# A seventh split step, denominators by square transposes and an earlier range check in the last image's second layer

## The chip, the cores and the metric

The kernel runs on one core of one Trainium2 chip. The metric is the device time of one execution in microseconds. The kernel before takes 3158.69 us, the median of three runs (3158.46 to 3160.62). One execution under the profiler took 3155.92 us, and its span in the trace, from the first to the last instruction, is 3154.1 us.

## The reference

Two attention layers, each with a residual, on four images of 4096 tokens and 256 channels, all in float32:

```python
# layer 0: q, k have 32 columns, v has 256
q, k, v = x @ Wq + bq, x @ Wk + bk, x @ Wv + bv
x = gamma * (softmax(q @ k.T) @ v) + x
# layer 1: f, g have 32 columns, v has 128; Wo brings 128 back to 256
f, g, v = x @ Wf + bf, x @ Wg + bg, x @ Wh + bh
out = x + (softmax(g @ f.T) @ v) @ Wo + bo
```

The softmax runs over the 4096 keys of the image. The kernel doesn't subtract a maximum: it takes exp of the scores, sums products and exponentials, and divides at the end. A range check at the end of the program counts denominators, values and gamma that are out of range; only if there are any does a general path run, and with these inputs it doesn't.

## The kernel before, in words

**Layers, blocks, steps.** For each image `b` and each layer `l` the queries are taken in blocks, and for each block the kernel goes through the keys in steps. In layer 0 a block has 256 queries and 8 steps of 512 keys (16 blocks). In layer 1, the one that is changed, a block has 512 queries and 16 steps of 256 keys (8 blocks, numbered 0 to 7 here). A class `Step` holds one step.

**One step of layer 1.** TensorE makes the scores `st` (L532): two products of 128 keys by 512 queries in the fast fp32r form. ScalarE takes the exponential from them, `p` (L544). TensorE then multiplies `p` with the values of these keys (L600), and the result adds up in PSUM over the steps of the block. This product comes in two forms.

- A *whole* step multiplies `p` by `v` in full float32, in two matmuls which stand as four in the trace.
- A *split* step, those in `SPLIT1`, does it in three products in fp32r, six matmuls in all. ScalarE also makes `high`, a slightly smaller exponential (L542); VectorE makes `low` from `p` and `high` (L555) and `d` from `low` and `high` (L560). The values have parts `h`, `l`, `d` of their own, made when the values are projected (L472 to L483). The products of `high` and `low` go to the accumulator acc0, those of `d` and of the whole steps to acc1.

**The denominators.** They are the sums of `p` over the keys. VectorE adds the `p` of eleven of the sixteen steps into `p_sum` (L571 the first two, L573 the others). The five steps of `MOVED_SUMS` are summed by accumulating transfers on GpSimd's queue (L548, L550) into a tile of tag "e".

**The end of a block.** ScalarE takes acc0 out into `o` (L651). `end_second` adds acc1 (L657), adds the moved sums to `p_sum` (L659) and halves it to `sums`, 128 partitions by 512 queries (L660): what is left is a sum over partitions. Then come four output units, one for each 128 queries, which run in the next block's steps 1 to 4: TensorE multiplies `o` by `Wo` (L667) and `sums` by a column of ones (L668), VectorE takes the reciprocal (L670), ScalarE scales (L673), and GpSimd's queue adds the result to the output in memory (L675).

**Buffers.** Tag "t" has two buffers, for `high` and `p` of split steps; tag "l" two, for `low` and `d`; tag "p" three, for `p` of whole steps; "d" and "e" one each, for the two sums; "small" four, among them those of `y`. In PSUM the scores of even and odd steps have one buffer each.

**What sets the order.** `plan` (L702 to L732) says at which step which units of the block before, and projections of the next image, are put. The loop over the steps (L735 to L802) writes a step as: `d` of this step, `low` of the next, the addition to `p_sum`, the scores of the step after the next (L775), the units of this step (L776), and the products of this step; the `d` product of a split step comes behind the product of the step after it (L778 to L783). The last step of a block takes acc0 out first (L774). The framework's scheduler then arranges the instructions of each engine from the dependencies and places in this order, so the built program's order is near to the written one and not the same.

**The end of the program.** After the last block's units the range check runs on VectorE: two comparisons and a product over all 256 columns of reciprocals, `inverse` (L808 to L810, in a "small" buffer), the check of values and gamma (L811 to L814), two reductions (L817), and then a count on TensorE (L821) which becomes the flag `off` (L822). The flag is read by the engines and a branch follows.

Of the kernel before, what the change touches and what calls it, by code (L numbers as in the profile page):

```python
# [57 lines left out]
P = 128  # L58
# [8 lines left out]

SPLIT1 = (0, 3, 5, 8, 11, 13)
MOVED_SUMS = (0, 4, 7, 9, 12)

# [168 lines left out]
def fast_path(ctx: ExitStack, tc: tile.TileContext, x, w0, w1, wo, bo, gamma, out, off):  # L239
# [11 lines left out]
    NI = (N // (G[0] * P), N // (G[1] * P))  # L251
    NS = QB0 // P
    NH = N // QB0
    split = [[l == 0 or i in SPLIT1 for i in range(NI[l])] for l in range(2)]
    V1 = NI[1] - sum(split[1])

    const = ctx.enter_context(tc.tile_pool(name="const", bufs=1))
    data = ctx.enter_context(tc.tile_pool(name="data", bufs=1))
# [30 lines left out]


    x_nat = {}
    LEAD_BUFS = sum(split[1])
    LEAD = V1 // NS

    def load_first(h):
# [11 lines left out]
    make_identity(nc, ident)  # L307
    ones = const.tile([P, 1], F32, name="ones")
    nc.vector.memset(ones, 1.0)

    inverse = const.tile([P, 2, B * N // P], F32, name="inverse")
    seen_v = const.tile([P, 2, B * NH], F32, name="seen_v")
# [99 lines left out]
    def project_units(b, l, h):  # L412

        key = (b, l, h)
        j, part = divmod(h, 2)
        cols = slice(part * QB0, (part + 1) * QB0)

        def qk_unit():
            ps = side_psum(f"psqk_{b}_{l}_{h}")[:, :QB0]
            for c in range(NCC):  # L420
                for n in range(2):
                    nc.tensor.matmul(  # L422
                        ps,
                        wqk[l][:, c, :],
                        x_parts[key][n][:, c, :],
                        start=(c == n == 0),
                        stop=(c == NCC - 1 and n == 1),
                    )
# [12 lines left out]
            nc.scalar.copy(parts[top, :], whole)  # L441
            nc.vector.tensor_sub(parts[bottom, :], whole, parts[top, :].bitcast(F32))

            if part == 0:
                qk_dram[b, l, j] = dram.tile([2, 2, D, QB], F32, name=f"qk_dram_{b}_{l}_{j}")
            nc.sync.dma_start(qk_dram[b, l, j].rearrange("h w d n -> (h w d) n")[:, cols], parts.bitcast(F32))
            halves[b, l, j] = part + 1
            if l == 0 and b > 0:
                load_half(b, h + 1)
            elif l == 1 and h == NH - 1:  # L450
                load_half(b + 1, 0)
            elif l == 1:
                load_squares((b, 1, h + 1), waiting.pop((b, h + 1)))
            if b == l == 0:
                near = parts.rearrange("(h w d) n -> h w d n", h=2, w=2)
                load_k(b, l, j, cols, near)
                if h == 0:
                    load_q(b, l, j, cols, near)

        def v_unit():  # L460
            ps = side_psum(f"psv_{b}_{l}_{h}")[:, : NS * CV[l]].rearrange("p (t c) -> p t c", c=CV[l])
            for t in range(NS):
                for c in range(NCC):
                    nc.tensor.matmul(  # L464
                        ps[:, t, :],
                        xT[key][:, c, t * P : (t + 1) * P],
                        wv[l][:, c, :],
                        start=(c == 0),
                        stop=(c == NCC - 1),
                    )  # L470
            seen = seen_v[:, l, b * NH + h : b * NH + h + 1]
            if split[l][h if l == 1 else 0]:  # L472
                if l == 0:
                    tiles = slice(part * NS, (part + 1) * NS)
                    high, low, d = (v0[j][what][:, tiles, :C] for what in ("h", "l", "d"))
                else:
                    t = data.tile([P, 3 * NS, P], F32R, tag="v1_parts", bufs=sum(split[1]), name=f"v_{b}_{h}")
                    high, low, d = (t[:, n * NS : (n + 1) * NS, :] for n in range(3))
                    v_t[b, h] = {"h": high, "l": low, "d": d}
                nc.scalar.activation(high, ps, AF.Copy, scale=1.0 - DOWN)  # L480
                nc.scalar.activation(low, ps, AF.Abs, accum_out=seen)
                nc.vector.scalar_tensor_tensor(d, high.bitcast(F32), -1.0 - EPS, ps, ALU.mult, ALU.add)
                nc.vector.scalar_tensor_tensor(low, d.bitcast(F32), UP, high.bitcast(F32), ALU.mult, ALU.add)  # L483
            else:
# [29 lines left out]
    class Step:  # L514


        def __init__(self, b, l, j, i):
            self.b, self.l, self.j, self.i = b, l, j, i
            self.first, self.last = i == 0, i == NI[l] - 1
            self.split = split[l][i]  # L520
            self.key = f"{b}_{l}_{j}_{i}"

        def scores(self):
# [18 lines left out]
                nc.scalar.activation(self.high, s_flat, AF.Exp, bias=down)  # L542
            self.p = wide("t" if self.split and l == 1 else "p", f"p_{self.key}")
            nc.scalar.activation(self.p, s_flat, AF.Exp)  # L544
            if l == 1 and i in MOVED_SUMS:
                if i == MOVED_SUMS[0]:
                    moved_sums[b, j] = wide("e", f"p_sum_moved_{b}_{j}")
                    nc.gpsimd.dma_start(moved_sums[b, j], self.p)  # L548
                else:
                    nc.gpsimd.dma_start(moved_sums[b, j], self.p, accum_op=ALU.add)  # L550
# [11 lines left out]
                )  # L562

        def add_up(self, p_sum):
            if self.l == 0 or self.i in MOVED_SUMS:
                return
            kept = [i for i in range(NI[1]) if i not in MOVED_SUMS]
            if self.i == kept[0]:
                first_p.append(self.p)
            elif self.i == kept[1]:  # L570
                nc.vector.tensor_add(p_sum, first_p.pop(0), self.p)  # L571
            else:
                nc.vector.tensor_add(p_sum, p_sum, self.p)  # L573
# [16 lines left out]
        def products_second(self, acc, parts):  # L590
            v = v_t[self.b, self.i]
            for part in parts:
                p, v_part, which, first, last = {
                    "h": lambda: (self.high, v["h"], 0, self.i == SPLIT1[0], False),
                    "l": lambda: (self.low, v["l"], 0, False, self.i == SPLIT1[-1]),
                    "d": lambda: (self.d, v["d"], 1, False, False),
                    "whole": lambda: (self.p, v, 1, self.i == 1, self.last),
                }[part]()
# [55 lines left out]
    def end_second(b, j, acc, p_sum, o):  # L654
# [3 lines left out]
        sums = work.tile([P, QB], F32, tag="sums", bufs=1, name=f"sums_{key}")  # L658
        nc.vector.tensor_add(p_sum, p_sum, moved_sums[b, j])  # L659
        nc.vector.tensor_add(sums, p_sum[:, :QB], p_sum[:, QB:])  # L660

        def output(t):
            def issue():
# [4 lines left out]
                nc.tensor.matmul(ps[:, C : C + 1], sums[:, tok], ones[:, :1], start=True, stop=True)  # L668
                n = (b * N + j * QB) // P + t
                nc.vector.reciprocal(inverse[:, 1, n : n + 1], ps[:, C : C + 1])  # L670
# [5 lines left out]

            return issue

        return [output(t) for t in range(NT)]

    def run(units):
        for u in units:
            u()


    x_res = {}
# [15 lines left out]
    def plan(b, l, j, ends):  # L702
# [3 lines left out]
        def put(i, *some):  # L706
            units.setdefault(i, []).extend(some)
# [15 lines left out]
        else:  # L723
            for n, u in enumerate(ends):
                put(1 + n, u)
        if b + 1 < B:
            for h in range(NH):
                i = 12 + 7 * h - j * NI[1]
# [72 lines left out]
        if s.last:  # L801
            ends = end_first(b, j, acc) if l == 0 else end_second(b, j, acc, p_sum, o)  # L802
    run(ends)

    good = small("good").rearrange("p (l n) -> p l n", l=2)
    nc.vector.tensor_scalar(good, inverse, 1.0 / SUM_MAX, None, ALU.is_ge)  # L808
    nc.vector.tensor_scalar(inverse, inverse, 1.0 / SUM_MIN, None, ALU.is_le)
    nc.vector.tensor_mul(good, good, inverse)  # L810
    nc.vector.tensor_scalar(seen_v, seen_v, VALUE_MAX, None, ALU.is_le)  # L811
    size = const.tile([P, 1], F32, name="size")
    nc.vector.tensor_mul(size, gamma_sb, gamma_sb)
    nc.vector.tensor_scalar(size, size, GAMMA_MAX**2, None, ALU.is_le)  # L814
    low = const.tile([P, 1], F32, name="low")
    for seen, axes in ((good, AX.XY), (seen_v, AX.XY)):
        nc.vector.tensor_reduce(low, seen, axes, ALU.min)  # L817
        nc.vector.tensor_mul(size, size, low)
    nc.vector.tensor_scalar(low, size, 1.0, None, ALU.is_lt)
    count = ps_side.tile([1, 1], F32, tag="side", name="count")  # L820
    nc.tensor.matmul(count, ones, low, start=True, stop=True)  # L821
# [51 lines left out]
```

## Time and profile before

| what | us |
|---|---|
| median of three runs | 3158.69 |
| the profiled execution | 3155.92 |
| its span in the trace | 3154.1 |
| TensorE busy | 3116.3 |
| VectorE busy | 2689.1 |
| ScalarE busy | 2140.1 |
| GpSimd busy | 900.7 |
| a block of the last image's second layer (`d` of step 0 at 3030.17, 3065.68, 3101.20) | 35.5 |
| from the flag (L822, starts at 3143.53) to the end of the span | 10.6 |

In the lines of the profile, PE is TensorE, PEld its loads of weights, which overlap its products, DVE VectorE, ACT ScalarE, POOL GpSimd and SP SyncE. A line of the timeline has a start and a duration in us, the engine, the line of the kernel, the operation, the tiles it writes and reads, their shapes, and how many instructions it stands for; square brackets give the idle time of the engine just before it and who ended it. A line of the groups has the busy time and the mean of one in ns, then the idle time before the group by who ended it. The rows of stretches have the busy time of each engine in that stretch, with its number of instructions.

The recorded duration of an instruction is a little longer than the distance from it to the next, since neighbours overlap; where costs are added up, it is done with these distances from start to start. The ends of matmuls are modelled.

### The profile page before, as it was taken

What the parts mean: (1) busy time and instruction counts of PE and PEld (TensorE: products, weight loads), DVE (VectorE), ACT (ScalarE), POOL (GpSimd) and SP (SyncE); (2) the same over time, 40 slices, a digit from 0 to 9 for tenths busy, and PEclk for the clock granted to TensorE, in tenths of its full rate; (3) what the DMA queues carried; (4) which work ended last, traced back from release to release, by engine and by line L of the source; (5) the groups of instructions that cost most, each with busy time, mean ns of one, the idle gap of its engine ahead of it and who ended that gap; (6) DMA issues with size and microseconds to landing.
All of it is one profiled execution on the core that took longest, in us unless ns stands there. A gap on an engine that the chain in (4) does not pass through costs nothing.

```text
span 3154.1 us, 54090 instructions
## 1 busy us (share of the span) xinstructions
PE 3116.3 (99%) x19908; PEld 2672.0 (85%) x19908; DVE 2689.1 (85%) x3237; ACT 2140.1 (68%) x2835; POOL 900.7 (29%) x1108
## 2 busy tenths in 40 slices
PE   8999999999999999999999999999999999999997
PEld 7999998666799999866679999976668999996664
DVE  7888888888888888888888888898888888888876
ACT  7666666777666666777766666677776666666674
POOL 5232224222422222422242222232223222233221
PEclk9999999999999999999999999999999999999999
DMA  4121114555512121555541112255554111125454
GB/s 119 43 53 47 48 48 104 107 108 105 104 44 51 41 53 47 113 101 112 107 93 47 49 45 51 51 116 107 105 113 81 48 46 47 49 65 105 97 95 73
DMA packets 391392, 239.49 MB, mean 76 GB/s; under 512 B 266672, under 2 KB 355248, under 8 KB 391120
## 3 DMA queue, kind: packets, MB, share of 16 engines
q0 software_dynamic: 68160, 134.86, 22.0%
q1 hardware_dynamic: 322048, 100.76, 13.4%
q8 instruction: 161, 2.64, 0.4%
q14 instruction: 111, 0.91, 0.1%
q10 hardware_dynamic: 912, 0.33, 0.1%
HBM read 82.58 MB, written 67.11 MB: 47 GB/s over the span
## 4 chain that ended last, share of the span: by engine, by line
PE 91%; DVE 3%; DMA 2%; issue 2%; ACT 1%; POOL 0%; SPq 0%; DVEq 0%; ACTq 0%; POOLq 0%
PE acc L600 24%; PE acc L582 23%; PE acc_pair L582 23%; PE st L532 14%; PE psv L464 4%; PE psqk L422 2%; PE pso L667 2%; DVE d L560 1%; DVE low L555 1%; ACT p L544 1%; DVE p_sum L573 1%; DMA p_sum_moved<-p 0%; DMA squares<-in_x 0%; PE pso L668 0%; DMA squares<-x_dram 0%
## 5 line engine op out<-in xcount | busy, mean ns | idle before, releaser
L542 ACT ACTIVATE high<-st,down 128x1024 fp32r<-128x1024 f32 x704 | 786.5, 1117 | 703.2 <-PE st L532 362.8
L544 ACT ACTIVATE p<-st 128x1024 f32<-128x1024 f32 x1024 | 1042.5, 1021 | 166.3 <-PE st L532 143.8
L560 DVE SCALAR_TENSOR_TENSOR d<-low,high 128x1024 fp32r<-128x1024 f32 x704 | 871.0, 1237 | 227.0 <-PE acc_pair L582 223.7
L555 DVE TENSOR_TENSOR low<-p,high 128x1024 fp32r<-128x1024 f32 x704 | 936.6, 1330 | 142.6 <-ACT p L544 141.6
L532 PE MATMUL st<-q,k 128*128 128x256 f32 (+1 forms) x3072 | 706.3, 338 | 2.5 <-DMA k<-qk_parts 1.4
L600 PE MATMUL acc<-p,v 128*128 128x512 f32 x1280 | 611.0, 597 | 0.0
L532 PEld LDWEIGHTS st<-q,k 128*128 128x128 f32 x3072 | 470.0, 189 | 103.3 <-issue 40.6
L639 POOL TENSOR_TENSOR x_res<-x,bo 128x256 f32<-128x256 f32 x128 | 212.5, 1660 | 879.3 <-DVE x L628 879.2
L600 PEld LDWEIGHTS acc<-p,v 128*128 128x128 f32 x1280 | 233.1, 189 | 161.8 <-issue 143.4
L573 DVE TENSOR_TENSOR p_sum<-p_sum,p 128x1024 f32<-128x1024 f32 x288 | 352.6, 1224 | 9.4 <-ACT p L544 5.8
L582 PE MATMUL acc<-v0h,high 128*128 128x258 f32 x2048 | 341.6, 284 | 1.2 <-ACT high L542 1.2
L582 PE MATMUL acc<-v0d,d 128*128 128x258 f32 x2048 | 339.2, 287 | 2.6 <-DVE d L560 2.2
L582 PE MATMUL acc<-v0l,low 128*128 128x256 f32 (+1 forms) x2048 | 329.3, 283 | 0.6 <-DVE low L555 0.5
L582 PE MATMUL acc_pair<-v0h,high 128*128 128x258 f32 x2048 | 329.8, 283 | 0.0
L582 PE MATMUL acc_pair<-v0l,low 128*128 128x256 f32 (+1 forms) x2048 | 328.8, 282 | 0.0
L582 PE MATMUL acc_pair<-v0d,d 128*128 128x258 f32 x2048 | 328.5, 282 | 0.0
L582 PEld LDWEIGHTS acc<-v0h,high 128*128 128x128 f32 x2048 | 286.0, 189 | 3.1 <-issue 1.4
L582 PEld LDWEIGHTS acc<-v0d,d 128*128 128x128 f32 x2048 | 281.5, 190 | 5.6 <-DVE d L560 4.9
L582 PEld LDWEIGHTS acc<-v0l,low 128*128 128x128 f32 x2048 | 282.2, 190 | 1.8 <-DVE low L555 1.3
L582 PEld LDWEIGHTS acc_pair<-v0h,high 128*128 128x128 f32 x2048 | 282.1, 189 | 0.0
L582 PEld LDWEIGHTS acc_pair<-v0l,low 128*128 128x128 f32 x2048 | 281.1, 189 | 0.0
L582 PEld LDWEIGHTS acc_pair<-v0d,d 128*128 128x128 f32 x2048 | 281.0, 189 | 0.0
(108 smaller groups left out, 3332.5 us busy)
## 6 DMA issues: line engine op xcount, KB each, us to landing
p_sum_moved<-p POOLq DMA_DIRECT2D x160, 512.0 KB, 4.7
x_res<-in_x SPq DMA_DIRECT2D x128, 128.0 KB, 2.1
qk_dram<-qk_parts SPq DMA_DIRECT2D x128, 128.0 KB, 1.9
x_dram<-x SPq DMA_DIRECT2D x128, 128.0 KB, 1.7
out<-x_res SPq DMA_DIRECT2D x128, 128.0 KB, 1.7
squares<-x_dram SPq DMA_DIRECT2D x512, 32.0 KB, 1.9
out<-y POOLq DMA_DIRECT2D x128, 128.0 KB, 3.2
q<-qk_dram POOLq DMA_DIRECT2D x252, 64.0 KB, 2.2
```

Source lines behind the costliest of these rows:

```text
L422: nc.tensor.matmul(ps, wqk[l][:, c, :], x_parts[key][n][:, c, :], start=(c == n == 0), stop=(c == NCC - 1 and n == 1),)
L464: nc.tensor.matmul(ps[:, t, :], xT[key][:, c, t * P : (t + 1) * P], wv[l][:, c, :], start=(c == 0), stop=(c == NCC - 1),)
L532: nc.tensor.matmul(st[:, g, :], k_t[b, l, kt // NT][:, kt % NT * P : (kt % NT + 1) * P], q_t[b, l, j * n // QB][:, q0 : q0 + n], start=Tru ...
L542: nc.scalar.activation(self.high, s_flat, AF.Exp, bias=down)
L544: nc.scalar.activation(self.p, s_flat, AF.Exp)
L555: nc.vector.tensor_sub(self.low, self.p, self.high.bitcast(F32))
L560: nc.vector.scalar_tensor_tensor(self.d, self.low.bitcast(F32), -UP, self.high.bitcast(F32), ALU.mult, ALU.add)
L573: nc.vector.tensor_add(p_sum, p_sum, self.p)
L582: nc.tensor.matmul(acc[2 * s + which][:, :width], p[:, g * QB0 + s * P : g * QB0 + (s + 1) * P], v0[self.i][v][:, g, :width], start=self.f ...
L600: nc.tensor.matmul(acc[which], v_part[:, g, :], p[:, g * QB : (g + 1) * QB], start=first and g == 0, stop=last and g == G[1] - 1,)
L639: nc.gpsimd.tensor_add(x_old[s], x_new[s], bo_sb)
L667: nc.tensor.matmul(ps[:, :C], part, wo_sb, start=True, stop=True)
```

## The change

In the last image's second layer, and only there:

- Steps 0, 3, 5, 8, 10, 12, 14 are split instead of 0, 3, 5, 8, 11, 13, and the sums that the transfers take are those of steps 0, 4, 7, 9, 11 instead of 0, 4, 7, 9, 12. The parts of the values of step 14 are stored in `v0[0]["h"]`, layer 0's values, which the last image no longer needs.
- In blocks 0 to 6 the denominators come another way. VectorE transposes `sums` in squares of 32x32, adds up each 32 columns (128x512 to 128x16), and one product on TensorE with `same` (a matrix of four by four identities of 32x32) adds the four groups of partitions; four reciprocals of 32x4 write all 512. The four products with ones and their reciprocals fall away. Block 7 keeps the old way.
- The range check is cut in two. The values, gamma and 252 columns of `inverse` are checked by a unit at step 13 of the last block, the last four columns at the end. Its scratch tile has tag "t" instead of "small".

At the start, seven small operations on GpSimd make `same`. The diff, cut to its core:

```diff
+SPLIT1_LAST = (0, 3, 5, 8, 10, 12, 14)
+MOVED_SUMS_LAST = (0, 4, 7, 9, 11)
...
+    same = const.tile([P, P], F32, name="same")
+    nc.gpsimd.tensor_copy(same[:, :S], ident[:, :S])
+    for a in range(1, P // S):
+        nc.gpsimd.tensor_add(same[:, :S], same[:, :S], ident[:, a * S : (a + 1) * S])
+    for a in range(1, P // S):
+        nc.gpsimd.tensor_copy(same[:, a * S : (a + 1) * S], same[:, :S])
...
-                    t = data.tile([P, 3 * NS, P], F32R, tag="v1_parts", bufs=sum(split[1]), name=f"v_{b}_{h}")
-                    high, low, d = (t[:, n * NS : (n + 1) * NS, :] for n in range(3))
+                    if h in splits(b)[:PARTS]:
+                        t = data.tile([P, 3 * NS, P], F32R, tag="v1_parts", bufs=PARTS, name=f"v_{b}_{h}")
+                    else:
+
+                        t = v0[0]["h"][:, : 3 * NS * P // C, :C].rearrange("p t (n c) -> p t n c", c=P)
+                        t = [t[:, n, :, :] for n in range(3)]
...
+        by_squares = b == B - 1 and j < NQ[1] - 1
+        if by_squares:
+
+            part_sums = work.tile([P, QB // S], F32, tag="part_sums", bufs=1, name=f"part_sums_{key}")
+            squares = p_sum[:, :QB]
+            nc.vector.transpose(squares, sums)
+            nc.vector.tensor_reduce(part_sums, squares.rearrange("p (n k) -> p n k", k=S), AX.X, ALU.add)
+
+        def denominators():
+
+            ps = side_psum(f"psd_{key}")[:, : QB // S]
+            nc.tensor.matmul(ps, same, part_sums, start=True, stop=True)
+            for a in range(P // S):
+                rows = slice(a * S, (a + 1) * S)
+                of_rows = ps[rows, :].rearrange("p (t a) -> p t a", a=P // S)[:, :, a]
+                nc.vector.reciprocal(inverse[rows, 1, n0 : n0 + NT], of_rows)
...
-                nc.tensor.matmul(ps[:, C : C + 1], sums[:, tok], ones[:, :1], start=True, stop=True)
-                n = (b * N + j * QB) // P + t
-                nc.vector.reciprocal(inverse[:, 1, n : n + 1], ps[:, C : C + 1])
+                n = n0 + t
+                if not by_squares:
+                    nc.tensor.matmul(ps[:, C : C + 1], sums[:, tok], ones[:, :1], start=True, stop=True)
+                    nc.vector.reciprocal(inverse[:, 1, n : n + 1], ps[:, C : C + 1])
...
-        return [output(t) for t in range(NT)]
+        return [denominators] * by_squares + [output(t) for t in range(NT)]
...
+    def check(values):
+        good = wide("t", f"good_{values.shape[1]}")[:, : values.shape[1]]
+        worst = work.tile([P, 1], F32, tag="g", name=f"worst_{values.shape[1]}")
+        nc.vector.tensor_scalar(good, values, 1.0 / SUM_MAX, None, ALU.is_ge)
+        nc.vector.tensor_scalar(values, values, 1.0 / SUM_MIN, None, ALU.is_le)
+        nc.vector.tensor_mul(good, good, values)
+        nc.vector.tensor_reduce(worst, good, AX.X, ALU.min)
+        nc.vector.tensor_mul(size, size, worst)
+
+    def check_all_but_last():
+        worst = work.tile([P, 1], F32, tag="g", name="worst")
+        nc.vector.tensor_mul(size, gamma_sb, gamma_sb)
+        nc.vector.tensor_scalar(size, size, GAMMA_MAX**2, None, ALU.is_le)
+        nc.vector.tensor_scalar(seen_v, seen_v, VALUE_MAX, None, ALU.is_le)
+        nc.vector.tensor_reduce(worst, seen_v, AX.XY, ALU.min)
+        nc.vector.tensor_mul(size, size, worst)
+        check(before_last_block)
...
+        if (b, j) == (B - 1, NQ[1] - 1):
+            put(NI[1] - 3, check_all_but_last)
...
     run(ends)
-
-
-
-    good = small("good").rearrange("p (l n) -> p l n", l=2)
-    nc.vector.tensor_scalar(good, inverse, 1.0 / SUM_MAX, None, ALU.is_ge)
-    nc.vector.tensor_scalar(inverse, inverse, 1.0 / SUM_MIN, None, ALU.is_le)
-    nc.vector.tensor_mul(good, good, inverse)
...
+    check(in_last_block)
```

In the same places `split`, `MOVED_SUMS` and `SPLIT1` are replaced by functions of the image, `splits(b)` and `moved(b)`.

More of the change, by code (lines that the diff above doesn't have):

```diff
@@ L253, in fast_path, with splits, moved @@
     NH = N // QB0
-    split = [[l == 0 or i in SPLIT1 for i in range(NI[l])] for l in range(2)]
-    V1 = NI[1] - sum(split[1])
+    PARTS = len(SPLIT1)
+    V1 = NI[1] - PARTS
+    def splits(b):
+        return SPLIT1_LAST if b == B - 1 else SPLIT1
+    def moved(b):
+        return MOVED_SUMS_LAST if b == B - 1 else MOVED_SUMS
     const = ctx.enter_context(tc.tile_pool(name="const", bufs=1))
@@ L291, in fast_path @@
     x_nat = {}
-    LEAD_BUFS = sum(split[1])
+    LEAD_BUFS = PARTS
     LEAD = V1 // NS
@@ L471, in v_unit @@
             seen = seen_v[:, l, b * NH + h : b * NH + h + 1]
-            if split[l][h if l == 1 else 0]:
+            if l == 0 or h in splits(b):
                 if l == 0:
@@ L476, in v_unit @@
                 else:
-                    t = data.tile([P, 3 * NS, P], F32R, tag="v1_parts", bufs=sum(split[1]), name=f"v_{b}_{h}")
-                    high, low, d = (t[:, n * NS : (n + 1) * NS, :] for n in range(3))
+                    if h in splits(b)[:PARTS]:
[3 more added lines that the diff above has]
+                        t = [t[:, n, :, :] for n in range(3)]
+                    high, low, d = t if isinstance(t, list) else (t[:, n * NS : (n + 1) * NS, :] for n in range(3))
                     v_t[b, h] = {"h": high, "l": low, "d": d}
@@ L519, in __init__ @@
             self.first, self.last = i == 0, i == NI[l] - 1
-            self.split = split[l][i]
+            self.split = l == 0 or i in splits(b)
             self.key = f"{b}_{l}_{j}_{i}"
@@ L544, in scores @@
             nc.scalar.activation(self.p, s_flat, AF.Exp)
-            if l == 1 and i in MOVED_SUMS:
-                if i == MOVED_SUMS[0]:
+            if l == 1 and i in moved(b):
+                if i == moved(b)[0]:
                     moved_sums[b, j] = wide("e", f"p_sum_moved_{b}_{j}")
@@ L564, in add_up @@
         def add_up(self, p_sum):
-            if self.l == 0 or self.i in MOVED_SUMS:
+            if self.l == 0 or self.i in moved(self.b):
                 return
-            kept = [i for i in range(NI[1]) if i not in MOVED_SUMS]
+            kept = [i for i in range(NI[1]) if i not in moved(self.b)]
             if self.i == kept[0]:
@@ L593, in products_second @@
                 p, v_part, which, first, last = {
-                    "h": lambda: (self.high, v["h"], 0, self.i == SPLIT1[0], False),
-                    "l": lambda: (self.low, v["l"], 0, False, self.i == SPLIT1[-1]),
+                    "h": lambda: (self.high, v["h"], 0, self.i == 0, False),
+                    "l": lambda: (self.low, v["l"], 0, False, self.i == splits(self.b)[-1]),
                     "d": lambda: (self.d, v["d"], 1, False, False),
@@ L660, in end_second @@
         nc.vector.tensor_add(sums, p_sum[:, :QB], p_sum[:, QB:])
+        n0 = (b * N + j * QB) // P
+        by_squares = b == B - 1 and j < NQ[1] - 1
[11 more added lines that the diff above has]
+                nc.vector.reciprocal(inverse[rows, 1, n0 : n0 + NT], of_rows)
         def output(t):
@@ L683, in run @@
             u()
+    size = const.tile([P, 1], F32, name="size")
+    flat = inverse.rearrange("p l n -> p (l n)")
+    before_last_block, in_last_block = flat[:, : 2 * B * N // P - NT], flat[:, 2 * B * N // P - NT :]
+    def check(values):
[14 more added lines that the diff above has]
+        check(before_last_block)
     x_res = {}
@@ L803, in fast_path @@
     run(ends)
-    good = small("good").rearrange("p (l n) -> p l n", l=2)
-    nc.vector.tensor_scalar(good, inverse, 1.0 / SUM_MAX, None, ALU.is_ge)
-    nc.vector.tensor_scalar(inverse, inverse, 1.0 / SUM_MIN, None, ALU.is_le)
-    nc.vector.tensor_mul(good, good, inverse)
[L811 to L814, printed above, removed]
+    check(in_last_block)
     low = const.tile([P, 1], F32, name="low")
-    for seen, axes in ((good, AX.XY), (seen_v, AX.XY)):
-        nc.vector.tensor_reduce(low, seen, axes, ALU.min)
-        nc.vector.tensor_mul(size, size, low)
     nc.vector.tensor_scalar(low, size, 1.0, None, ALU.is_lt)
```

## The prediction, made before the changed kernel ran

> **What bounds the kernel now.** I began with the busy shares on the page.
>
> ```profile
> PE 3116.3 (99%) x19908; PEld 2672.0 (85%) x19908; DVE 2689.1 (85%) x3237; ACT 2140.1 (68%) x2835; POOL 900.7 (29%) x1108
> ```
>
> TensorE is full and VectorE not far behind. An average says little of one stage, so next come busy times by stretch for the last image's second layer, the only stage that the change touches (columns: stretch, length, then PE, PEld, DVE, ACT, POOL).
>
> ```profile
> 2950.00:3000.00 50.00, 50.00 (x177) 32.06 (x175) 41.76 (x46) 34.30 (x41) 13.43 (x20) 1.00 0.47 95
> 3050.00:3100.00 50.00, 50.00 (x173) 31.65 (x172) 40.27 (x42) 34.31 (x41) 10.45 (x14) 1.00 0.47 88
> ```
>
> TensorE is never idle here: a microsecond of its work removed is a microsecond won, so long as nobody makes it wait. The groups of this stage (2910 to 3100, shapes apart) show who has slack: busy time and mean, then idle time before, with its releaser.
>
> ```profile
> L544 ACT ACTIVATE p<-st 128x1024 f32<-128x1024 f32 x87 | 88.5, 1025 | 35.5 <-PE st L532 35.5
> L555 DVE TENSOR_TENSOR low<-p,high 128x1024 fp32r<-128x1024 f32 x33 | 40.4, 1224 | 35.5 <-ACT p L544 35.5
> L560 DVE SCALAR_TENSOR_TENSOR d<-low,high 128x1024 fp32r<-128x1024 f32 x32 | 39.0, 1218 | 0.0
> ```
>
> TensorE releases ScalarE, which releases VectorE: about 1.1 us of waiting per split step (35.5/33) is the slack of the chain. The timeline at a block's end shows where it is spent (start, duration, engine, line).
>
> ```profile
> 3093.97 0.62 PE L600 MATMUL acc<-low,v 128*128 128x512 f32 x2
> ...
> 3094.64 0.65 ACT L651 ACTIVATE o<-acc 128x256 f32<-128x256 f32 x2
> 3094.89 1.88 PE L600 MATMUL acc<-p,v 128*128 128x512 f32 x4
> 3095.17 1.12 ACT L542 ACTIVATE high<-st,down 128x1024 fp32r<-128x1024 f32 x1
> ...
> 3096.21 1.03 PE L600 MATMUL acc<-d,v 128*128 128x512 f32 x2
> 3097.07 0.63 PE L532 MATMUL st<-q,k 128*128 128x512 f32 x2
> 3097.54 1.88 PE L600 MATMUL acc<-p,v 128*128 128x512 f32 x4
> ...
> 3098.86 1.03 PE L532 MATMUL st<-q,k 128*128 128x512 f32 x2
> 3099.72 0.63 PE L600 MATMUL acc<-high,v 128*128 128x512 f32 x2
> ```
>
> The last `low` product of a block closes acc0; ScalarE empties it (L651) and writes `high` of the next block; only then may the next block's `high` product overwrite acc0. Six groups of products lie between (two whole steps, three score products, one `d`), from 3094.43 to 3099.72: 5.3 us, while `high` is done at 3096.2. So nobody waits. The end of the program:
>
> ```profile
> 3135.10 0.69 DVE L660 TENSOR_TENSOR sums<-p_sum 128x512 f32<-128x512 f32 x1
> ...
> 3138.50 0.17 DVE L670 RECIPROCAL inverse<-pso 128x1 f32<-128x1 f32 x1 [0.49 <-PE pso L668]
> ...
> 3140.65 0.29 DVE L808 TENSOR_SCALAR good<-inverse 128x256 f32<-128x256 f32 x1 [1.99 <-DMA out<-y]
> ...
> 3143.53 0.15 DVE L822 CAST off<-count 1x1 int32<-1x1 f32 x1 [0.37 <-PE count L821]
> ```
>
> From the last reciprocal to the flag it is 5.03 us, 1.99 of it a wait for an output transfer, because `good` reuses a `small` buffer.
>
> **What the Trainium skill says.** "TensorE: Matmul & The Clock Gate", Architectural detail: TensorE's queue only pulls weight loads ahead of matmuls in flight, and ScalarE and VectorE take instructions strictly in order. The trace agrees: PEld overlaps, matmuls start in program order. So a product that waits holds all behind it. "Perfetto Trace Analysis", Optimization Strategy: a gap that recurs on the engine that should be saturated can mean too few SBUF or PSUM buffers for the next tile. Before shows no such gap here (50.00 of 50); I expect one after. "VectorE: DVE Perf Modes", The three transpose paths: VectorE transposes 32x32 blocks separately, hence one product with `same` to finish the sums; the trace has such a transpose of 128x512 at L392, 704 ns.
>
> **Prices**, start to start from these timelines: fp32r pair 0.46 us; a whole step's four matmuls 1.72; L667 pair 0.43, L668 pair 0.23; ACT `high` 1.01, `p` 0.90, the pair of `o` 0.54; DVE `low`, p_sum and `d` 1.14 each. The start of the last `low` product to `o` is 0.67; a score product's end to ACT about 0.25; the other handovers 0.02 to 0.1.
>
> **The change part by part**, in the order in which the built program's instructions stand.
>
> TensorE's work. A step in three products costs 6 matmuls of 0.23, 1.38, against 1.72: -0.34 a block. The denominators drop four pairs of 0.23 and add one 16-column product; the trace has none, the L668 pair of one column is the nearest: 0.1 to 0.23, I take 0.2. So -0.72 in each of blocks 0 to 6. Its work per block falls from 35.52 (`d` of step 0 at 3030.17, 3065.68, 3101.20) to 34.45.
>
> VectorE's work. The seventh split adds `low` and `d`, 2.28. The transpose adds 0.70; the reduction of 128x512 is priced from L817's 0.42 for 128x256: 0.6 to 0.84, I take 0.7; the reciprocals change little. About +3.6 a block on about 28.6 (40.27/50 of 35.52): 32.2 of 34.45, busy 93%. Cover: `d` of step 0 goes ahead of the transpose, and the product is due some 0.8 later than the reduction ends, so I cost denominators at nothing on VectorE; without that cover, 0.5 a block.
>
> The chain. Splits now stand at 8, 10, 12, 14 and 16 (the next block's 0), all two apart. Tag "t" has two buffers for `high` and `p`: in the built order a split's `high` waits for the previous split's p_sum, and its `p` for the previous split's `d`. The round is p 0.90, low 1.14, p_sum 1.14, d 1.14 and handovers, 0.2 to 0.3: about 4.6, where TensorE needs 1.38+0.46+1.72+0.46, 4.0, for two steps. One such pair (3 to 5, 11 to 13) is absorbed now by three-step gaps around it; four in a row lose 2.4. I walked this from the score product of step 6: p6, high5, p5 end at 3.1; low5, p_sum, d5 at 6.6; low8 to d8 at 11.1; low10 to d10 at 15.5; p13, p12, low12 to d12 at 20.7; p14, p_sum 13, low14 at 23.0 to 23.4. TensorE's work up to there is 22.7. So the chain's slack is spent and it waits 0.3 to 0.7 at the last `low` product.
>
> The boundary. That product now stands at step 14, and the built order puts only step 3's scores (0.46) between it and the first half of the next block's `high` product; `d` of step 14 and the last whole product are queued behind it on TensorE, and VectorE's L657 and the next block's whole products (they wait for acc1) behind those. From its start: 0.67 to `o`, 0.54, high 1.01, handover 0.1: 2.32, less 0.92 of work: 1.4 waited per block, where 5.3 us of products covered it before. Then step 4's scores wait for p of step 2, whose scores come after those delayed products: 0.25+0.90+0.1 less 0.7 of cover, 0.6. Together 2.3 to 3.3; I take 2.8.
>
> Period: 34.45+2.8 = 37.2, +1.7 on 35.52. Six periods, 1 to 7: +10.2. Block 0 to 1 is longer now (37.2, with leftover projections) and gets the same end: +1.8.
>
> The check's other part (L811 to L818 for the values and gamma, some six operations of 0.15 to 0.3, about 1.1 us) moves to VectorE in block 0, which its leftover projections stretch anyway: nothing; 1.1 if VectorE is late there.
>
> The last block has no denominators by squares, and keeps the step's edit: `d` of step 14 in front of the last whole product, low14 late, and the 252-column check, whose `good` takes a "t" buffer and so stands behind `d` of step 14 on VectorE, ahead of L659 and L660, which the last products wait for (L808, L809, L810, L817: 0.29+0.29+0.43+0.42 = 1.4). From `low` of step 8 to L660 I get 19.75 for 15.86: +3.9. Then four columns are checked instead of 256 and no transfer is waited for: last reciprocal to flag about 1.98 for 5.03, -3.05. Net +0.85. If VectorE were free, the check would hide and the tail gain be -3.
>
> Startup. `same` is seven small GpSimd operations among its bias loads; L364 waits 0.67 for gamma, at 12.81. Cost 0 to 1, taken 0.3. Output transfers keep their queue and SyncE's order is the same. Step 14's parts lie in v0[0]["h"], free in the last image; its conversion swaps forms only: nothing.
>
> Sum: 10.2+1.8+0.85+0.3 = +13.2. The profiled execution took 3155.92, so 3169.1 after; the median of the runs stands 2.77 above it: 3171.9, say 3172.
>
> **The rivals.** A, as above: the latency chain takes TensorE's place. Own range 3167 to 3179 (2.8 plus or minus 0.8 per block).
> C: the chain has more slack than I walk, and only the boundary counts, 1.4+0.6 less 1.07 saved: +0.95 a block, 6.6+0.85+0.3 = +7.8: 3166.5. For it: 35.5 us of idle before `low` now.
> B, the other side: the built order leaves enough work between the last `low` product and the next `high`, or the handovers overlap, so TensorE stays full and the change does what it says: -1.07 x 7 - 0.34 - 3 = -10.8: 3148. It decides when waits per block are under 1.07. For it: 50.00 of 50 now; against it: the 2.32 us latency with 0.92 of cover.
> D: the moved sums (a transfer of some 4 us after L659, before `high` of step 3 may take its buffer) or the wait for the denominators bite too: another 1.2 a block: 3180.
>
> **How the numbers follow.** A 0.57, C 0.20, B 0.13, D 0.10. The likeliest gives 3172. Of 8 in 10 the range must leave out B and the far end of D: 3161 to 3182; C's lower end, with waits of 1.5 a block, sets the bottom. About 0.2%, 6.3 us, is what a measurement can tell here. Faster by more than that: B's body, 0.12; within: B's rest and C's lower half, 0.10; slower 0.78.
>
> **What would show it.** A: period 37 and PE at 46 to 47 of 50 us in this stage; idle before L600's `high` product released by ACT `high` L542's line, about 1.4 a block; idle before `low` products released by DVE; no wait before L808's successor on a transfer. B: 50 of 50 and period 34.4. Wrong altogether if the first three images' times move, since their order is the same.

## The result, and the profile after

The changed kernel takes 3181.18 us, the median of six runs (3178.89 to 3184.14), against 3158.57 us for the kernel before: the ratio is 1.0073, 95% interval 1.0061 to 1.0086, or 19 to 27 us more. Forecast were 3172 and a range of 3161 to 3182. The profiled execution took 3178.99 us with a span of 3177.2, which is 23.1 more than before. In the profiles after, lines have moved by 23 to 56: L542 and L544 are now L565 and L567, L555, L560 and L573 are L578, L583 and L596, L532 is L555, L600 is L623, L651 is L674, L822 is L878.

First the page's busy shares, then three stretches of the last image's second layer, with the same columns as before.

```profile
PE 3126.3 (98%) x19882; PEld 2667.7 (84%) x19882; DVE 2713.4 (85%) x3274; ACT 2150.5 (68%) x2843; POOL 911.3 (29%) x1115
```

```profile
2950.00:3000.00 50.00, 48.25 (x162) 29.28 (x162) 41.30 (x43) 34.08 (x38) 13.32 (x19) 1.00 0.50 95
3000.00:3050.00 50.00, 46.50 (x155) 27.54 (x154) 44.19 (x49) 32.99 (x38) 11.01 (x15) 1.00 0.39 79
3050.00:3100.00 50.00, 48.26 (x162) 29.33 (x161) 42.14 (x46) 34.19 (x40) 13.94 (x18) 1.00 0.55 96
```

TensorE, full before, now waits. The 1.7 to 3.5 us of 50 understate it: a matmul's record overlaps the next one's (a pair of fp32r products is recorded as 0.62 us, and the next pair starts 0.46 after it), so gaps of a few tenths vanish. The number of instructions in a stretch says more: 155 to 162, where the two stretches shown for before have 177 and 173. The groups of this stretch (2935 to 3120) name what is new; the first line is that of `high` before (2910 to 3100).

```profile
L542 ACT ACTIVATE high<-st,down 128x1024 fp32r<-128x1024 f32 x32 | 35.7, 1117 | 24.0 <-PE st L532 16.1 <-DVE inverse L670 7.9
...
L578 DVE TENSOR_TENSOR low<-p,high 128x1024 fp32r<-128x1024 f32 x35 | 42.9, 1225 | 26.9 <-ACT p L567 26.6
...
L565 ACT ACTIVATE high<-st,down 128x1024 fp32r<-128x1024 f32 x34 | 37.9, 1116 | 17.3 <-DVE p_sum L596 11.2 <-PE st L555 6.1
...
L623 PE MATMUL acc<-high,v 128*128 128x512 f32 x59 | 21.5, 419 | 4.7 <-ACT high L565 4.7
```

Before, `high` was released by TensorE's scores, and for a third of its idle time by a reciprocal of the output units; never by `p_sum`. Now VectorE's sum releases it for 11.2 of 17.3 us: that is the tag "t" buffer which the `p` of the split before still holds. And products of `high` wait for ScalarE, which none did before. The timeline at the end of block 5 shows the latter; its first two lines are the `low` products of steps 10 and 12.

```profile
3067.54 0.62 PE L623 MATMUL acc<-low,v 128*128 128x512 f32 x2
...
3072.21 0.71 PE L623 MATMUL acc<-low,v 128*128 128x512 f32 x2
...
3076.80 0.74 PE L623 MATMUL acc<-low,v0h 128*128 128x512 f32 x2 [0.30 <-DVE low L578]
3077.57 0.66 ACT L674 ACTIVATE o<-acc 128x256 f32<-128x256 f32 x2
...
3077.61 0.73 PE L555 MATMUL st<-q,k 128*128 128x512 f32 x2
...
3078.11 1.12 ACT L565 ACTIVATE high<-st,down 128x1024 fp32r<-128x1024 f32 x1
...
3079.28 0.50 PE L623 MATMUL acc<-high,v 128*128 128x512 f32 x1 [0.94 <-ACT high L565]
...
3079.62 0.62 PE L623 MATMUL acc<-d,v0h 128*128 128x512 f32 x2
...
3080.08 1.88 PE L623 MATMUL acc<-p,v 128*128 128x512 f32 x4
...
3083.54 0.73 PE L555 MATMUL st<-q,k 128*128 128x512 f32 x2 [0.42 <-ACT p L567]
```

This is the boundary of the prediction, in its order: the last `low` product is late by 0.30; only step 3's scores stand between it and the next block's `high` product, which waits 0.94 by the record (1.2 counted from where the scores' cost ends); `d` of step 14 and the last whole product, done when it lets them, are behind it; step 4's scores wait 0.42. The rounds ahead of it are long too: from one `low` product to the next it is 4.67 us (step 10 to 12) and 4.59 (12 to 14), where the round before, from step 8 (3063.50), took 4.04. The end of the program:

```profile
3163.36 0.17 DVE L713 RECIPROCAL inverse<-pso 128x1 f32<-128x1 f32 x1 [0.49 <-PE pso L712]
3163.56 0.17 DVE L737 TENSOR_SCALAR good<-inverse 128x4 f32<-128x4 f32 x1
...
3165.38 0.15 DVE L878 CAST off<-count 1x1 int32<-1x1 f32 x1 [0.37 <-PE count L877]
```

From the last reciprocal to the flag it is 2.02 us instead of 5.03; nothing waits for a transfer there.

Where the 23.1 us of the two profiled executions lie (`low` product of step 8 to that of the next block for periods):

| stretch | before | after | difference | forecast |
|---|---|---|---|---|
| start to `low` product of step 8, block 0 | 2868.99 | 2871.83 | +2.8 | +0.3 |
| block 0 to 1 | 37.2 | 40.1 | +2.9 | +1.8 |
| six periods, block 1 to 7, each | 35.51 | 37.90 | +14.3 | +10.2 |
| step 8 of block 7 to its `sums` | 15.86 | 20.65 | +4.8 | +3.9 |
| last reciprocal to flag | 5.03 | 2.02 | -3.0 | -3.05 |
| flag to end | 10.6 | 11.8 | +1.2 | 0 |

The seven operations that make `same` don't explain the first row: after the first image the two stand 0.4 apart, and 2.6 after the third, though up to there TensorE and ScalarE have the same instructions in the same order. The last `sums` of the third image stand anywhere from 2395.1 to 2402.9 in the twelve profiles here whose kernels are alike up to there but for those seven (all but e8).

### The profile page after: what moved, and what is told of

Its sections match the earlier page's. It is cut to its first block, busy times and chain, and to the rows that moved or that the text cites. A ratio compares the mean times of both kernels' runs of the same rounds, so it can differ in the third digit from the quotient of the medians.

```text
span 3177.2 us, 54069 instructions
## 1 busy us (share of the span) xinstructions
PE 3126.3 (98%) x19882; PEld 2667.7 (84%) x19882; DVE 2713.4 (85%) x3274; ACT 2150.5 (68%) x2843; POOL 911.3 (29%) x1115
## 4 chain that ended last, share of the span: by engine, by line
PE 92%; DVE 3%; ACT 2%; issue 2%; DMA 1%; POOL 0%; SPq 0%; DVEq 0%; ACTq 0%; POOLq 0%
PE acc L623 23%; PE acc L605 23%; PE acc_pair L605 23%; PE st L555 14%; PE psv L482 4%; PE psqk L440 2%; PE pso L709 2%; ACT p L567 1%; DVE low L578 1%; DVE p_sum L596 1%; DVE d L583 1%; ACT high L565 0%; PE pso L712 0%; DMA squares<-in_x 0%; DMA p_sum_moved<-p 0%
## 5 line engine op out<-in xcount | busy, mean ns | idle before, releaser
L565 ACT ACTIVATE high<-st,down 128x1024 fp32r<-128x1024 f32 x712 | 796.1, 1118 | 701.1 <-PE st L555 347.9
L567 ACT ACTIVATE p<-st 128x1024 f32<-128x1024 f32 x1024 | 1042.2, 1022 | 166.1 <-PE st L555 141.7
L583 DVE SCALAR_TENSOR_TENSOR d<-low,high 128x1024 fp32r<-128x1024 f32 x712 | 879.8, 1236 | 234.4 <-PE acc_pair L605 231.4
L578 DVE TENSOR_TENSOR low<-p,high 128x1024 fp32r<-128x1024 f32 x712 | 942.7, 1324 | 135.6 <-ACT p L567 134.1
L555 PE MATMUL st<-q,k 128*128 128x256 f32 (+1 forms) x3072 | 709.6, 339 | 6.1 <-ACT p L567 4.2
L623 PE MATMUL acc<-p,v 128*128 128x512 f32 x1248 | 597.0, 597 | 0.0
L555 PEld LDWEIGHTS st<-q,k 128*128 128x128 f32 x3072 | 467.1, 189 | 114.2 <-issue 42.5
L623 PEld LDWEIGHTS acc<-p,v 128*128 128x128 f32 x1248 | 228.9, 190 | 155.8 <-issue 136.2
L596 DVE TENSOR_TENSOR p_sum<-p_sum,p 128x1024 f32<-128x1024 f32 x288 | 352.9, 1225 | 5.8 <-ACT p L567 3.4
```

The source lines that it names most:

```text
L555: nc.tensor.matmul(st[:, g, :], k_t[b, l, kt // NT][:, kt % NT * P : (kt % NT + 1) * P], q_t[b, l, j * n // QB][:, q0 : q0 + n], start=Tru ...
L578: nc.vector.tensor_sub(self.low, self.p, self.high.bitcast(F32))
L583: nc.vector.scalar_tensor_tensor(self.d, self.low.bitcast(F32), -UP, self.high.bitcast(F32), ALU.mult, ALU.add)
L623: nc.tensor.matmul(acc[which], v_part[:, g, :], p[:, g * QB : (g + 1) * QB], start=first and g == 0, stop=last and g == G[1] - 1,)
```

## The experiments

All ratios are to the kernel before, run beside each kernel. "Period" is from one block's `sums` to the next in the last image's second layer (35.51 before, 37.90 after), without the first and the last block; a range is given where the blocks differ.

| run | splits | period us | ratio | 95% interval |
|---|---|---|---|---|
| changed kernel | 7, last at 14 | 37.90 | 1.0073 | 1.0061 to 1.0086 |
| e1_den_check | 6 | 35.30 | 0.9994 | 0.9986 to 1.0002 |
| e2_split | 7, last at 14 | 38.3 to 39.6 | 1.0079 | 1.0065 to 1.0093 |
| e3_check | 6 | 35.51 | 0.9997 | 0.9988 to 1.0005 |
| e4_high_bufs | 7, last at 14 | 35.55 | 1.0008 | 1.0000 to 1.0016 |
| e5_six14 | 6, last at 14 | 35.4 to 35.7 | 1.0003 | 0.9994 to 1.0012 |
| e6_seven13 | 7, last at 13 | 39.35 | 1.0090 | 1.0073 to 1.0107 |
| e7_high_noden | 7, last at 14 | 36.20 | 1.0015 | 1.0008 to 1.0022 |
| e8_t3p2 | 7, last at 14 | 36.4 to 39.6 | 1.0056 | 1.0039 to 1.0072 |
| e9_best6 | 6 | 35.43 | 0.9994 | 0.9986 to 1.0002 |
| e10_best7 | 7, last at 14 | 35.52 | 0.9999 | 0.9991 to 1.0007 |
| e11_best7_13 | 7, last at 13 | 34.75 | 0.9980 | 0.9973 to 0.9987 |

**The parts, one at a time.** Without the seventh split (e1):

```diff
-SPLIT1_LAST = (0, 3, 5, 8, 10, 12, 14)
-MOVED_SUMS_LAST = (0, 4, 7, 9, 11)
+SPLIT1_LAST = SPLIT1
+MOVED_SUMS_LAST = MOVED_SUMS
```

> The seventh split is taken back: in the last image's second layer the splits are 0, 3, 5, 8, 11, 13 and the moved sums 0, 4, 7, 9, 12, as before; denominators by squares and the early range check stay. Theory A (the chain over the two tag-t buffers, which the five splits two apart bring): no chain, so TensorE stays full at 50 of 50 us and the block's period falls from 35.5 to 34.8 (three products of 0.23 fewer, net); with 2 to 3 us from the end about 3151 us. Rival V (VectorE's added work, transpose and reduction 1.4 us a block, is what costs): the period is no shorter than 35.5, 3157 to 3167 us.

The loss is gone: 35.30. So it is the seventh split that costs. The period lies between theory A's 34.8 and rival V's 35.5, though: the denominators save 0.21 a block here, not the 0.72 that I expected. Of TensorE's waits in 2935 to 3100, two are new or larger than before:

```profile
PEld acc L623 <- DVE d L583: 2.9, 9, 0.4
...
PEld psd L698 <- DVE part_sums L693: 1.8, 4, 0.5
```

The output product that stood in front of step 1's product is behind the reduction now, and gives no cover any more while `d` and the reduction are made.

The seventh split alone (e2), with the old denominators and the old check:

> The seventh split alone, with its moved sums; denominators and range check as before. Theory A: the chain sets the period, and neither the products nor VectorE's transposes that are taken out matter: the period stays near 37.9 us, and with the longer end 3181 to 3185 us. Rival V: 1.4 us of VectorE's work a block come back, period 36.5, about 3173 us. If the two causes add, between them.

The period is 38.35 in the first three of these blocks, then 38.7 and 39.6; in the first of these two the granted clock falls to half for 3.4 us (from 3081.05). The time is 3186.25, against 3159.91 for the kernel before. Taking 1.4 us of work off VectorE wins nothing: rival V falls, and the cost is the split's own.

The check alone (e3):

> The earlier range check alone. All theories: the end from the last reciprocal to the flag falls from 5.0 to 2.0 us; theory A has 252 columns checked behind VectorE's slack, so 3155 to 3157 us; if the check's 1.4 us stand on the path to the last products, 3157 to 3158 us.

No difference that can be measured, and the profile says why. VectorE at the end of this kernel:

```profile
3135.69 0.41 DVE L733 TENSOR_REDUCE worst<-good 128x1 f32<-128x252 f32 x1
3136.01 0.41 DVE L673 TENSOR_TENSOR o<-o,acc 128x256 f32<-128x256 f32 x1
...
3138.87 3.54 POOL L711 DMA_DIRECT2D out<-y  x4 [12.49 <-ACT y L709]
```

The check stands ahead of L673 (L657 before) on VectorE: the last block is 0.8 longer. The flag then comes 3.0 sooner after the last reciprocal (at 3142.16), but GpSimd is still issuing the last output transfers until 3142.4, and from the flag to the end it is 11.3 instead of 10.6 us. -3.0+0.8+0.7 leaves a gain of 1.5 us, too little for these medians. In the two profiles in which GpSimd had been done 2.7 us before the flag (before and e2), it is 10.6 and 10.7 from the flag to the end, and in the other eleven 11.1 to 12.0. That the engines' common branch waits for GpSimd is argued, not shown.

**Buffers or VectorE** (e4). The values of layer 0 are not needed any more, and each tile holds one `high`:

```diff
-                self.high = wide("t", f"high_{self.key}", F32R)
+                if l == 1 and b == B - 1:
+                    at = splits(b).index(i)
+                    self.high = v0[1 + at % 3]["hld"[at // 3]].rearrange("p t c -> p (t c)")[:, : 2 * QB]
+                else:
+                    self.high = wide("t", f"high_{self.key}", F32R)
```

> The changed kernel with one edit: in the last image's second layer `high` of the seven splits lies in seven tiles of layer 0's values, which are free by then, so that the two tag-t buffers are left to `p`. Theory A: `high` no longer waits for the sum of the split before, nor `p` for its `d`; `high` of the next block stands behind the last whole product in the built order; period 34.5 to 35.5 us and 3150 to 3162 us. Rival V: VectorE's work is the same, so the period stays at 37 to 38 us and the time at 3176 to 3182 us.

The period falls to 35.55 and the time to 3163.46 (3159.91 for the kernel before), both just above what theory A allowed and far below rival V; VectorE has the same work and is busy 45 of 50 us. `high` is released by the scores alone:

```profile
L569 ACT ACTIVATE v0l<-st,down 128x1024 fp32r<-128x1024 f32 x15 | 16.7, 1115 | 12.9 <-PE st L555 12.9
...
L569 ACT ACTIVATE v0h<-st,down 128x1024 fp32r<-128x1024 f32 x13 | 14.5, 1118 | 14.9 <-PE st L555 14.9
```

The edit takes two things away at once, the waits on tag "t" and the order which the scheduler had made because of them: the next block's `high` product stands behind the last whole product again. Together they are 37.90-35.55 = 2.35 us a block. How this divides between them is not shown. It left a wait at the boundary, of step 2's scores for `p` of step 0, which ScalarE makes behind `high` of that step:

```profile
3065.34 1.12 ACT L569 ACTIVATE v0h<-st,down 128x1024 fp32r<-128x1024 f32 x1 [1.09 <-PE st L555]
...
3066.36 1.01 ACT L571 ACTIVATE p<-st 128x1024 f32<-128x1024 f32 x1
...
3067.43 0.49 PE L555 MATMUL st<-q,k 128*128 128x512 f32 x1 [0.72 <-ACT p L571]
```

With the old denominators beside it (e7):

> Seven splits at the changed kernel's places, `high` in seven tiles of layer 0's values as in the run before, early check, but the denominators by four products with ones as before (1.4 us less of VectorE's work a block, 0.8 us more of TensorE's). If what is left in that run's period of 35.5 us is VectorE's lateness at the block's end: the two cancel, 35.2 to 35.6 us, 3160 to 3164 us. If TensorE alone set it: 36.3 us, 3168 us.

36.20: the products that were taken off TensorE count, and the denominators are worth 0.65 a block here.

More buffers in another way (e8): three for tag "t", two for tag "p".

> The changed kernel with three buffers of tag t and two of tag p (in all images), the code otherwise the same: another way to ease the waits between rounds. If the waits on the two tag-t buffers are the cause: the last image's period falls most of the way, to 35.5 to 36.5 us, unless the missing third buffer of `p` costs as much; the first three images' second layers show that cost alone (0 to 1 us a block). If buffers are not the cause: 37.9 us and more.

It tells nothing of the cause. The periods run from 36.4 to 39.6, with another halved clock in the longest. `p` of whole steps now waits for the transfers that sum it, ScalarE's largest wait in 2935 to 3110 (26.2 us in 13 waits). In the first three images' second layers the missing buffer costs at most 0.2 a block, so what it costs in the last image can't be read from them.

**The run of rounds or the place at 14.** Six splits with the last at 14 (e5), and seven with five rounds two apart but the last at 13 (e6):

```diff
+SPLIT1_LAST = (0, 3, 5, 8, 11, 14)        # e5, moved sums 0, 4, 7, 9, 12
+SPLIT1_LAST = (0, 3, 5, 7, 9, 11, 13)     # e6, moved sums 0, 4, 8, 10, 12
```

> Denominators and early check stay; six splits again, at 0, 3, 5, 8, 11, 14 in the last image's second layer (moved sums 0, 4, 7, 9, 12). The last split stands at 14, two steps before the next block's first, as in the changed kernel, but no run of splits two apart leads to it. If the run of four rounds over the two tag-t buffers is the cause: period 35.3 us as with 13 (that run had 35.30), about 3158 us. If the place at 14, next to the block's end, is enough by itself: period 36.5 to 37.5, 3167 to 3173 us.

> The changed kernel with seven splits at 0, 3, 5, 7, 9, 11, 13 (moved sums 0, 4, 8, 10, 12): five rounds two apart, but three steps between the last split and the next block's first. If the run of rounds is the cause: they lose 4 times about 0.6 us before the last `low` product and the next block's `high` product waits, period 36.5 to 38.5, 3167 to 3182 us. If the place at 14 is the cause: period 35.0 to 35.5, 3155 to 3160 us.

The place alone costs 0.1 to 0.4 a block against 35.30; the longer run costs more than the changed kernel's, 39.35, and more than the 36.5 to 38.5 expected. A part of it may be of another kind: in e6 `p` also waits 1.2 us a block for a transfer of the moved sums, which it does neither in the changed kernel nor in e11. One round can be read off e6's VectorE (two `low` and, between, what ScalarE waited for):

```profile
3042.36 1.22 DVE L578 TENSOR_TENSOR low<-p,high 128x1024 fp32r<-128x1024 f32 x1 [1.15 <-ACT p L567]
...
3046.95 1.22 DVE L578 TENSOR_TENSOR low<-p,high 128x1024 fp32r<-128x1024 f32 x1 [1.09 <-ACT p L567]
```

```profile
3044.84 1.11 ACT L565 ACTIVATE high<-st,down 128x1024 fp32r<-128x1024 f32 x1 [2.51 <-DVE p_sum L596]
```

3046.95-3042.36 = 4.6 us, the round that the prediction added up and the two that the changed kernel shows above. It needs no other engine to be full: ScalarE waits 2.51 us in it and VectorE 1.1.

**A version that beats both.** Three kernels with the end units one step later and the early check at step 7 of the last block, its scratch in a free tile of layer 0's values: six splits (e9), the changed kernel's seven (e10), seven with the last at 13 (e11); in e10 and e11 `high` lies as in e4.

```diff
-                put(1 + n, u)
+                put(1 + n + (b == B - 1), u)
...
-            put(NI[1] - 3, check_all_but_last)
+            put(7, check_all_but_last)
...
-        good = wide("t", f"good_{values.shape[1]}")[:, : values.shape[1]]
+        free = v0[0]["l" if values.shape[1] > NT else "d"]
+        good = free.rearrange("p t c -> p (t c)")[:, : values.shape[1]]
```

> Six splits as before, denominators by squares with every end unit put one step later, early check put at step 7 of the last block and its scratch in a free tile of layer 0's values instead of tag t (so it waits for nothing). If the early check costs only by where it stands ahead of the last sums: the last block's excess of 0.8 us goes, and with the end 2 us shorter and periods of 35.2 us the time is 3 to 5 us below before. If the products that wait for VectorE's reduction still do: period 35.3 us and 2 to 4 us below.

> Seven splits at the changed kernel's places, `high` in tiles of layer 0's values, end units one step later, early check at step 7 as in the run beside it. If the denominators' product, due too early, made the remaining waits in the run with `high` elsewhere (35.5 us): period 34.6 to 35.2 us and 3 to 8 us below before. If the order at the block's end does (`p` of step 1 behind `high` of step 0 on ScalarE): period 35.2 to 35.6 us, within 3 us of before.

> The same with seven splits at 0, 3, 5, 7, 9, 11, 13 (moved sums 0, 4, 8, 10, 12), three steps between the last and the next block's first. Theory A: with tag t left to `p` the run of rounds costs nothing, where with two buffers it gave 39.35 us; period 34.5 to 35.2 us, 5 to 10 us below before. If rounds two apart bind by themselves (VectorE's 3.4 us a round and ScalarE's order), 36 us and more.

e11 is 0.2% faster than before, 3154.31 against 3160.24 us, and its period of 34.75 is what theory A gave. TensorE is full:

```profile
2950.00:3000.00 50.00, 50.00 (x175) 31.94 (x173) 46.65 (x50) 35.50 (x42) 12.99 (x19) 1.00 0.50 100
3050.00:3100.00 50.00, 50.00 (x173) 32.16 (x172) 46.19 (x47) 35.16 (x42) 11.29 (x15) 1.00 0.50 93
```

The same split places that gave 39.35 with the two tag "t" buffers (e6) give 34.75, though VectorE is busy 93% of the time; two steps take 4.03 us there (`low` products at 3051.21 and 3055.24). e10 differs from e11 in the places of the splits and moved sums alone: with the waits on tag "t" gone, the changed kernel's places cost 35.52-34.75 = 0.77 a block. TensorE's wait of 0.7 us for `p` at the boundary, seen in e4, is in each of five blocks of e10 and in none of e11, so that is where they cost it. It is near the second case of e10's forecast, which named `p` of step 1. Later end units won nothing (35.52 for e4's 35.55). The early check costs nothing in the last block of e10 and e11, which is 0.8 and 1.0 shorter than the period, as before (34.51 for 35.51). In e9 it is 0.2 longer, which I missed, and the time is 1.4 us below before, too little to be told from none; ScalarE waits 1.6 for a moved sum there, and whether that is the cause wasn't tried.

## Why the prediction was right, and where its size was off

**What bounds, and the sign: right.** TensorE was full before, and waits brought by the seventh split set the time after. Rival B's point, waits under 1.07 us a block, is far passed.

**The size: inside the range by 0.8 us.** The rise was forecast as 13 and is 23. Theory A's own range, 3167 to 3179, is missed by 2 us; the stated one reached to 3182 because it took in the near part of rival D, which is not what happened. That the number fell inside is in part luck.

**The chain: right in kind, too small ahead of the last `low` product.** A round of 4.6 us was forecast, and the changed kernel has 4.67 and 4.59. Against the 4.03 that two steps take in e11, these two rounds lose 1.2 us a block, where the walk through the chain gave 0.3 to 0.7. From the last `low` product to the next `high` product it is 2.48 us (3076.80 to 3079.28); less the same 0.92 of work, 1.6 waited for 1.4. Step 4's scores wait 0.4 for 0.6. Together these are 3.2, and 37.90-34.75 = 3.15 is what the changed kernel has above e11, where TensorE is full by the record. I took 2.8. But the prediction's three terms add up to 2.3 to 2.7 and not to the 2.3 to 3.3 that it says: the error in the sum hid some of the error in the first term.

By the experiments, the waits on tag "t" with the order they bring are 2.35 us a block (e4) and the places of the splits 0.77 (e10 and e11). The place at 14 alone costs 0.1 to 0.4 in six splits (e5), so the boundary's wait needs the late chain in front of it.

**TensorE's work: mis-sized.** 34.45 was forecast and e11, full, has 34.75. The denominators' 0.72 comes down to 0.21, 0.45 or 0.65 (e1, the changed kernel against e2's 38.35, e4 against e7). The lists of waits put 0.3 to 0.5 us a block on the reduction in e1, e4 and e11: it is not ready when its product is due. That this is the whole difference isn't shown. It is the 0.5 a block that I named for the case without cover, and costed at nothing. 0.3 too little for work and 0.3 for waits make 0.65 a block, 4 us of the 10 that the sum is short.

**The last block: 4.8 for 3.9.** The places are right, but one cost was not thought of: the granted clock, below. It made VectorE wait 1.07 us for the last product, so without it the block would have come to some 3.7. **Startup and drift:** 2.5 of the 10 are no part of the change. The prediction called itself wrong altogether if the first three images' times moved; they moved by 2.6 us, but kernels alike up to there differ by 7.8, so that sign was too strict. **The end:** -3.0 to the flag is right, but 1.2 comes back between flag and end, for which there was no term.

**The rivals.** C was too small. D's 3180 is the nearest number, but not for its reason: in the wait lists of the changed kernel's stage, no ScalarE or TensorE wait is put down to a transfer, and the wait for the denominators is 0.7 us in five blocks.

## What to carry to other kernels

When a product form gives TensorE less to do but ScalarE and VectorE more, add up the round in which a buffer comes back, and compare it with TensorE's time for the same steps. One round that is too long was absorbed here by the gaps around it; four in a row were not, and being below 100% on every other engine said nothing of this. Look for memory that is dead in this phase before giving the form up: seven dead tiles turned +0.7% into +0.1% (e4), and other places for the splits made it -0.2% (e11).

## What the hardware showed that I had not expected

The last block of the changed kernel, by stretches of 2 us: TensorE waits for `low` and then for `d` of step 14 (1.05 and 1.54 us idle), and in the columns after POOL the granted clock follows.

```profile
3152.00:3154.00 2.00, 0.73 (x2) 0.30 (x2) 2.00 (x3) 0.63 (x2) 0.00 (x0) 1.00 0.00 0
3154.00:3156.00 2.00, 1.13 (x3) 0.67 (x4) 2.00 (x3) 0.03 (x1) 0.00 (x0) 0.93 0.00 0
3156.00:3158.00 2.00, 2.00 (x4) 0.67 (x2) 1.82 (x4) 0.00 (x0) 0.00 (x0) 0.50 0.00 0
3158.00:3160.00 2.00, 1.42 (x4) 0.58 (x4) 1.10 (x5) 0.00 (x0) 0.00 (x0) 0.72 0.00 0
```

```profile
3155.44 3.35 PE L623 MATMUL acc<-p,v 128*128 128x512 f32 x4
```

The clock is halved for some 3.4 us, and falls on the last product: 3.35 us where it took 1.88 before. The Trainium skill, "TensorE: Matmul & The Clock Gate", What's actually happening, has the two clocks and the window of 3.4 us; the trace agrees with both. The page speaks of an idle window, and here TensorE worked for 1.56 of the 3.41 us ahead of it (3152.29 to 3155.70). So this wait on VectorE was paid twice: it also thinned out TensorE's work, and the clock fell. It fell in the middle of the stage too, in e2 after 1.84 us of work in 3.41 and in e8 after 1.40. What share of work is enough to keep the clock isn't shown.
